# Dividing exponentials in plain column order, with a planner that knows the GpSimd port

## The chip, the cores and the metric

The kernel runs on one core of a Trainium2 chip. A core has five engines that take their instructions in order, each from its own queue: TensorE (PE in the profile, with its weight loads shown as PEld), VectorE (DVE), ScalarE (ACT), GpSimd (POOL), and SyncE (SP), which here only starts DMAs. The metric is the time of one execution on the device in microseconds; the time given for a kernel is the median of its runs.

## The reference

The input is a batch of 32 sequences of 256 tokens with 256 features, in fp32. Each sequence goes through a cross attention with 16 heads of 16 features between the sequence `x` and the side input, with a mask by length and one extra key per query (its own), then through a two-layer transformer, and the result is added to `x`. Cut to what matters here, a layer is:

```python
h = shift_token(x)                       # second half of the features from the token before
q, k, v = split(h @ wqkv)                # 8 heads of 64
q, k = rotary(l2norm(q) * qs, l2norm(k) * ks)
sim = q @ k.T                            # own window of 128 tokens and the one before, causal
attn = softmax(where(mask, -inf, sim))   # exponentials, divided by their sum
x = x + (attn @ v) @ wo
h = layernorm(shift_token(x)) * lg + lb
a, g = split(h @ w1 + b1)
x = x + (a * gelu(g)) @ w2 + b2
```

The change touches the division in `softmax`.

## The kernel before, in words

The 32 sequences are worked off in 16 groups of two. The kernel does not write its instructions out directly. It first records them in a `Plan`: a *unit* is a stretch of TensorE work (with a tiling of the array: `full`, or 2 or 4 tiles by `rows` or by `cols`), and each instruction on another engine is a *node* that hangs on a unit. `Plan.run` then plays the whole program through with prices per instruction (`price`), delays from engine to engine (`HOP`), buffers of each pool, the eight PSUM banks among them, and picks at each moment which unit TensorE takes next. What it picks decides the order in which `Plan.issue` emits all instructions, on all engines; that order is then kept. All instructions are emitted at one line, 567 of the kernel before, so the profile's groups differ by tile names, not by lines.

The choice among units that are ready is a score in `policy`: the unit's place in a nominal schedule (`u.stand`, from a `PERIOD` for each group, a stretch, and a number per unit from the tables `SHIFT`, `FIRST` for the first group and `FINAL` for the last two), a price for a change of tiling (`SWITCH`), a price for a backlog on the engines that it feeds, and a bonus for feeding them (`FEED`, capped by `MOST`), and a price on banks (`BANKS`). A unit that is marked soft (a full-size product) is emitted in column tiles when it follows a unit in column tiles, so the order also decides in how many pieces a product is issued. Copies recorded on `either` go to VectorE or ScalarE, whichever the plan finds free first. A table load is added on ScalarE whenever its functions need another table.

The names that matter below:
- In the cross attention: `cq`, `ck`, `cs`, `vals` are projections, `self` a small product (8 columns), `S` the scores (their row maxima `mx` are taken on VectorE), `nmT` their transposes, `ST` the scores again in the other orientation, `eT` their exponentials, `AV` the weighted sums, `ohT`, `turn` transposes, `co` the output projection.
- In a layer's attention: `q`, `k`, `v` projections; `sq`, `rot`, `raw`, `ss`, `rq` the norm and the rotation (the products `raw<-raw,rot` and `raw<-raw,ss` and the powers `rq`, `ss` run on GpSimd); `qkT` transposes; `sc` the scores; `ex` the exponentials; `exT` their transposes; `av` the weighted sums; `wout` the output projection.
- In the feed-forward part: `mean`, `var` (1 column), `rs`, and `w` for the products with `w1` and `w2`.

The function `weights` makes the exponentials of two heads: the masked maximum on VectorE out of PSUM (`ex<-sc,misc`), the product of maximum and scale (`nm<-nm,rq`), the exponential on ScalarE with its sum (`den`), the reciprocal, and the division by the sum, in place in SBUF, on VectorE. The division goes through the columns in strided order: of 256 columns, or of 128, it takes one from each half in turn.

```python
part = (
    es[:, i, 1:3, :].rearrange("p k q -> p q k")
    if w
    else es[:, i, 0, :].rearrange("p (k q) -> p q k", k=2)
)
vec.tensor_scalar(part, part, den[:, i, w : w + 1], None, ALU.mult)
```

Of the kernel before, what the change touches and what calls it, by code (L numbers as in the profile page):

```python
# [14 lines left out]
AF = mybir.ActivationFunctionType  # L15
ALU = mybir.AluOpType
# [6 lines left out]
G = 2  # L23
# [125 lines left out]
class Node:  # L149


    def __init__(self, engine, unit, number):
        self.engine, self.unit, self.number = engine, unit or self, number
        self.ops, self.cost, self.table, self.load = [], 0.0, None, 0.0
        self.after, self.then, self.ready, self.tiles = {}, [], 0.0, set()


class Plan:
# [15 lines left out]
    def __init__(self, tc, engines, pools, make):  # L174
        self.tc, self.engines, self.pools, self.make = tc, engines, pools, make
        self.nodes, self.units, self.unit_, self.group, self.place = [], [], None, 0, 0.0
        self.stage, self.stages, self.done = 0, {}, set()


    def tile(self, pool, name, shape):  # L180
# [52 lines left out]
    def record(self, engine, name, args, kw):  # L233
# [6 lines left out]
        if engine == "PE":  # L240
            node, wide = u, int(np.prod(out.shape[1:]))
            u.soft = u.soft and name == "matmul" and kw["lhsT"].shape[1] == 128
            cost = (2 if name == "transpose" else 4) * (wide + 2) / 2400 / u.streams
            if name == "transpose" and u.streams > 1:
                cost = max(cost, 0.062 / u.streams)
            cost = max(cost, 0.2) if wide < 64 else cost
            u.small += wide < 64
            turn = 0.65 if name == "transpose" else 1.0 if wide >= 64 else 0.0
            u.weight += cost * turn * self.WORK.get(u.kind, 1.0)
            u.place += cost  # L250
            self.place += cost
        else:
            node = self.node(engine, u)
            self.edge(u, node)
            if name == "dma_start":

                dst, src = kw["out"].shape, kw["in_"].shape
                run = min(dst[-1], src[-1])
                cost, node.load = 0.55, int(np.prod(dst)) / run * max(0.048, run * 4 / 24e3) / 16
            else:  # L260
                cost, node.table = self.price(engine, name, args, kw, size)
                if engine == "X":
                    node.either = {"V": cost, "S": 0.068 + size / 1267}
                u.feeds[engine] = u.feeds.get(engine, 0.0) + cost
# [10 lines left out]
    def price(self, engine, name, args, kw, size):  # L275

        if engine in "VX":
            extra = 0.02 if name == "reciprocal" else 0.0
            if name == "scalar_tensor_tensor":
                extra = 0.06  # L280
            return 0.065 + extra + size / 960, "any" if engine == "X" else None
        if engine == "S":
            func = args[2] if name == "activation" else None
            table = "exp" if func is AF.Exp else "gelu" if func is AF.Gelu else "any"
            extra = 0.315 if "accum_out" in kw else 0.11 if table == "gelu" else 0.0
            extra += 0.09 if func is AF.Identity else 0.0
            return 0.068 + size / 1267 + extra, table
        power = any(v is ALU.pow for v in args)
        return (0.35 + 0.158 * size if power else 0.1 + (0.00187 if size <= 256 else 0.00215) * size), None

# [3 lines left out]
    def run(self, policy):  # L294
# [4 lines left out]
        units, self.backlog = [], {e: 0.0 for e in "VSGDX"}  # L299
        left = {n: len(n.after) for n in self.nodes}  # L300
        self.kind, self.table, pe, blocked = ("full", 1), "any", 0.0, 0.0
        self.begin()
        self.tick, self.filled, self.warm = 0, 0.0, False
        for n in self.nodes:
# [3 lines left out]
        for u in self.units:  # L308
            for tiles in u.takes.values():
                for t in tiles:  # L310
                    t.lead = u.cost if t.lead is None else t.lead
                tiles.sort(key=lambda t: t.lead)
        self.idle = self.switches = self.cold = self.wire = 0.0

        def put(n):
            if n.engine == "PE":
# [40 lines left out]
        while todo:  # L357
# [12 lines left out]
            if e != "PE":  # L370
                ready = [n for n in waiting[e] if n.ready <= t]
                n = min(ready, key=lambda n: self.rank(n, e))
                waiting[e].remove(n)
                cost = n.cost
                if e == "S" and n.table not in ("any", None, self.table):
                    self.table, cost = n.table, cost + 1.3
                now[e] = t + cost
# [3 lines left out]
                todo -= 1  # L381
                end = t + cost
                if n.load:
                    self.wire = max(self.wire, end) + n.load
                    end = self.wire + self.LANDING
                ended(n, end)
                continue
            fit = {u: fits(u) for u in units if u.ready <= t}
# [148 lines left out]

    def rank(self, n, e):
        other = e == "S" and n.table not in ("any", None, self.table)
        return n.ready + 2.0 * other, n.number  # L540


    def parted(self, u):
# [8 lines left out]
    def issue(self, order):  # L552
# [7 lines left out]
        for n in order:  # L560
# [3 lines left out]
            for name, args, kw in ops:  # L564
                if n.engine in "VS" and name == "copy":
                    name = "tensor_copy" if n.engine == "V" else "copy"
                ins = getattr(self.engines[n.engine], name)(  # L567
                    *[real(v) for v in args], **{k: real(v) for k, v in kw.items()}
                )
# [3 lines left out]
class Engine:  # L573
# [12 lines left out]


SHIFT = [
    156, 528, 54, -76, 49, 292, -28, 245, 120, -102, -425, 52, -30, 35, 68, 22, 33, 22, -208,
    -4, 119, -41, 61, 69, 90, 152, 19, 32, -62, -238, 52, -2, 49, -168, 13, -85, -54, -65, 36,  # L590
    64, 112, -439, -349, -167, 223, -408, -5, 62, -46, -234, 56, -27, 119, -7, -45, 96, -17,
    -38, 61, -374, -335, -58, 1, -150, -372, -152, -51, -265, -409, 8, 67, -53, 114, -41, -17,
    -83, 34, 68, 48, 60, -261, -99, -7, -76, -335, -100, -105, -191, -306, -58, 15, -102, 32,
    -23, -66, 39, -309, -188, 106, -258, 33, -30, -139, 22, -141, 82, -290, -255, 32, 19, -99,
    134, 126, 14, -15, -222, -574, -156, 97, 93, -32, -241, 50, 152, -118, -41, -45, 21, -102,
    20, 47, 3, 15, 55, 169, -56, -24, 43, 199, -247, 143, -97, -15, -223, -41, -95, -88, -212,
    -127, -29, -32, -285, -545, -142, -265, -8, -118, -6, 152, 84, -122, 25, 14, 4, 18, 141, 60,
    166, -454, -139, 25, -127, -186, -20,
]
FIRST = [  # L600
    0, 0, 0, 0, 0, 0, 0, 0, 10, 35, -9, 213, 102, 95, 210, -345, -65, -122, -290, 49, -201, 6,
    -193, -61, -7, 106, 99, -6, -100, -16, 106, 13, 65, -266, -137, 7, -58, 247, 58, 69, 48, 1,
    -114, -155, -32, -173, -34, 65, 135, 130, -117, 69, 71, 117, 272, 156, 73, -3, -1, -31, -33,
    -133, 51, 151, 175, 239, 445, 215, 231, 120, 135, 97, -3, -90, -188, -357, -32, -64, -276,
    -297, -374, -330, -535, -346, -72, -135, -217, 156, 27, 182, 40, -174, -48, 77, -252, -118,
    -307, -246, 33, -96, -400, -238, -150, -69, -239, 6, 79, 152, 26, -38, -60, -358, -15, -155,
    89, -99, -69, -60, 87, -3, -114, -222, -118, 60, -143, -246, -29, -171, -319, -115, -49,
    -17, -96, -75, -88, 113, 144, -56, -6, 35, -9, -141, -41, -74, -183, -115, -131, -49, -79,
    109, -65, -145, 55, -88, -244, -157, -153, -264, -181, -118, -121, -82, -23, -37, -86, -83,
    -110, -213, -219, -209, -160, -63, 0, 0,  # L610
]
FINAL = [
    0, 0, 0, 0, 0, 0, 0, 0, 56, -34, 24, 16, 12, 140, -55, -63, -14, 1, -33, -84, -66, -53, -46,
    -145, -40, -121, 67, -19, -32, -29, 98, 97, 8, 45, -119, -130, -61, -106, 67, 94, -33, 8,
    54, 33, 8, -94, -222, -47, -210, -95, -90, -11, -121, 156, 49, 10, 43, 87, 7, 64, -144, -81,
    35, -80, 47, -31, -76, -182, 53, 86, 32, 67, 229, 49, 115, 31, 6, -10, -135, 40, 27, -79,
    -83, -8, 108, -110, 63, -40, -249, -98, -95, -18, -170, -139, -28, -12, -41, 76, 83, 116,
    59, -9, 65, -157, -74, -50, -119, -145, -16, -25, 13, 6, 73, -2, -181, -184, -151, -49, -97,
    116, -8, 56, 187, 15, 69, -31, -42, -59, 109, 161, 193, 112, 209, 211, 117, 80, 41, 59, 77,
    -84, 136, 47, 92, -54, 145, 66, 93, 1, -60, 152, -30, 108, 108, -119, 50, -9, -29, -39, 44,  # L620
    -113, -118, -128, -103, 66, 10, -89, -27, -49, -2, -10, 53, 34, -67, -8,
]


# [1 line left out]
def tile_kernel(ctx: ExitStack, tc: tile.TileContext, a: dict, out: bass.AP):  # L626
# [415 lines left out]
    def attention(l, b, res):  # L1042
# [80 lines left out]
        def weights(c, sc):  # L1123
# [29 lines left out]
                        accum_out=den[:, i, w : w + 1],  # L1153
                    )
            vec.reciprocal(den, den)

            for i in range(2):
                for w in range(2):
                    part = (
                        es[:, i, 1:3, :].rearrange("p k q -> p q k")  # L1160
                        if w
                        else es[:, i, 0, :].rearrange("p (k q) -> p q k", k=2)
                    )
                    vec.tensor_scalar(part, part, den[:, i, w : w + 1], None, ALU.mult)
            return es

        def turned(ess):
# [209 lines left out]
    STRETCH, AHEAD, LAST = 2.75, 3, 14  # L1377
    AGE, SWITCH, OVER, STAY, ENTER = 0.02, 1.5, 1.0, 6.0, 4.0
    HURRY = 0.0
    FEED, MOST, BANKS = 1.0, 3.0, 0.0  # L1380


    numbers = {}
# [68 lines left out]
```

## Time and profile before

| what | value |
|---|---|
| median of three runs | 3427.64 us (3423.55 to 3428.22) |
| the profiled execution's own time | 3422.27 us |
| its span, first to last instruction | 3420.5 us |
| mean granted TensorE clock | 0.990 |
| TensorE busy | 3348.6 us (98%) |
| VectorE busy | 2161.9 us (63%) |
| ScalarE busy | 1780.5 us (52%) |
| GpSimd busy | 1163.4 us (34%) |
| ScalarE table loads | 96, 1283 ns each |

A group of the profile is one kind of instruction with its tiles: busy time, mean duration, and the engine's idle time before them. A busy TensorE is not one at its peak, since the ends of matmuls are modelled; the distance from the start of one matmul to the start of the next says more. An fp32 product appears as two records in the profile, a transpose as one.

### The profile page before, as it was taken

What the parts mean: (1) busy time and instruction counts of PE and PEld (TensorE: products, weight loads), DVE (VectorE), ACT (ScalarE), POOL (GpSimd) and SP (SyncE); (2) the same over time, 40 slices, a digit from 0 to 9 for tenths busy, and PEclk for the clock granted to TensorE, in tenths of its full rate; (3) what the DMA queues carried; (4) which work ended last, traced back from release to release, by engine and by line L of the source; (5) the groups of instructions that cost most, each with busy time, mean ns of one, the idle gap of its engine ahead of it and who ended that gap; (6) DMA issues with size and microseconds to landing.
All of it is one profiled execution on the core that took longest, in us unless ns stands there. A gap on an engine that the chain in (4) does not pass through costs nothing.

```text
span 3420.5 us, 69279 instructions
## 1 busy us (share of the span) xinstructions
PE 3348.6 (98%) x25984; PEld 1908.7 (56%) x25984; DVE 2161.9 (63%) x6673; ACT 1780.5 (52%) x4537; POOL 1163.4 (34%) x1195
## 2 busy tenths in 40 slices
PE   6999999999999999999999999999999999999998
PEld 5665556465564655656455564655646556465554
DVE  3558567485675747657485674847657486574763
ACT  0556456473554726456373563735547364554653
POOL 0325052250613407043160522507134070432541
PEclk7999999999999999999999999999999999999999
DMA  5100010010101001010010100101010010100001
GB/s 147 20 15 11 12 27 9 16 26 9 26 15 21 17 13 20 16 20 17 13 21 14 27 13 15 24 7 26 16 20 17 13 20 15 27 15 12 4 2 27
DMA packets 310926, 69.00 MB, mean 20 GB/s; under 512 B 286776, under 2 KB 308096, under 8 KB 310592
## 3 DMA queue, kind: packets, MB, share of 16 engines
q1 hardware_dynamic: 298848, 54.24, 9.3%
q10 hardware_dynamic: 11744, 10.34, 1.1%
q8 instruction: 207, 3.39, 0.4%
q14 instruction: 127, 1.04, 0.1%
HBM read 35.53 MB, written 8.39 MB: 13 GB/s over the span
## 4 chain that ended last, share of the span: by engine, by line
PE 77%; DVE 12%; POOL 3%; ACT 1%; issue 1%; POOLq 0%; SPq 0%; DMA 0%; DVEq 0%; ACTq 0%
PE w L567 27%; DVE ex L567 6%; PE wout L567 6%; PE q L567 5%; PE av L567 4%; PE k L567 4%; PE sc L567 4%; PE S L567 4%; PE v L567 3%; PE ST L567 3%; PE vals L567 3%; PE AV L567 3%; PE exT L567 2%; PE qkT L567 2%; DVE rot L567 2%; PE cs L567 2%
## 5 line engine op out<-in xcount | busy, mean ns | idle before, releaser
L567 ACT ACTIVATE ex<-ex,nm,rq 128x128 f32<-128x128 f32 (+1 forms) x1024 | 546.2, 537 | 107.3 <-DVE nm L567 106.1
L567 PE MATMUL w<-cen,w 128*128 128x512 f32 (+2 forms) x1480 | 589.2, 598 | 0.8 <-DVE cen L567 0.3
L567 POOL TENSOR_TENSOR raw<-raw,rot 128x512 f32<-128x512 f32 x256 | 327.6, 1281 | 749.2 <-DVE rot L567 660.3
L567 PEld LDWEIGHTS w<-cen,w 128*128 128x128 f32 (+2 forms) x1480 | 224.9, 175 | 270.7 <-issue 231.4
L567 DVE TENSOR_SCALAR ex<-ex,den 128x128 f32<-128x128 f32 (+1 forms) x1024 | 351.4, 457 | 5.2
L567 DVE TENSOR_REDUCE mx<-S 128x2 f32<-128x512 f32 x512 | 314.3, 686 | 49.4 <-PE S L567 49.3
L567 PE MATMUL w<-act,w 128*128 128x512 f32 (+3 forms) x880 | 324.6, 602 | 2.9 <-DVE act L567 2.8
L567 ACT ACTIVATE eT<-ST 128x512 f32<-128x512 f32 x512 | 263.8, 605 | 115.0 <-PE ST L567 109.8
L567 DVE CUSTOM_DVE_ANT_0 ex<-sc,misc 128x128 f32<-128x128 f32 (+1 forms) x1024 | 299.2, 353 | 31.3 <-PE sc L567 30.8
L567 DVE SCALAR_TENSOR_TENSOR act<-w,b,act 128x512 f32<-128x512 f32 (+1 forms) x192 | 143.4, 748 | 262.0 <-PE w L567 195.5
L567 ACT ACTIVATE act<-w,b 128x512 f32<-128x512 f32 (+1 forms) x192 | 128.9, 686 | 280.1 <-PE w L567 276.8
L567 POOL TENSOR_TENSOR xs<-stream 128x512 f32<-128x512 f32 x32 | 35.0, 1094 | 641.5 <-PE cs L567 318.1
L567 PE MATMUL wout<-qT,wout 128*64 128x256 f32 (+2 forms) x1728 | 242.8, 381 | 0.5 <-DVE nm L567 0.3
L567 PE MATMUL v<-wqkv,stream 128*128 128x512 f32 (+1 forms) x608 | 242.5, 599 | 0.0
L567 PE MATMUL k<-wqkv,stream 128*32 128x512 f32 (+2 forms) x1104 | 239.9, 593 | 0.0
L567 PE MATMUL q<-wqkv,stream 128*32 128x512 f32 (+2 forms) x960 | 237.7, 594 | 0.2 <-ACT stream L567 0.2
L567 ACT COPY exT<-exT 128x384 f32<-128x384 f32 x512 | 207.3, 498 | 54.5 <-PE exT L567 53.8
L567 PEld LDWEIGHTS w<-act,w 128*128 128x128 f32 (+3 forms) x880 | 124.8, 176 | 167.1 <-issue 151.5
L567 POOL TENSOR_TENSOR rq<-ss,minus_half 128x8 f32<-128x8 f32 x128 | 215.1, 1684 | 4.9
L567 POOL TENSOR_TENSOR ss<-ss,minus_half 128x8 f32<-128x8 f32 x128 | 213.3, 1666 | 5.7
L567 PE MATMUL sc<-kT,qT 64*128 64x128 f32 (+1 forms) x2048 | 205.7, 337 | 0.4
L567 PEld LDWEIGHTS wout<-qT,wout 128*64 128x64 f32 (+2 forms) x1728 | 161.6, 147 | 73.0 <-issue 17.6
(127 smaller groups left out, 5520.2 us busy)
## 6 DMA issues: line engine op xcount, KB each, us to landing
ft<-in_fside_BxSxS_dram SPq DMA_DIRECT2D x128, 64.0 KB
xt<-in_x_dram SPq DMA_DIRECT2D x128, 64.0 KB
qh<-qc SPq DMA_DIRECT2D x256, 32.0 KB
kh<-kc SPq DMA_DIRECT2D x256, 32.0 KB
ot<-in_x_dram SPq DMA_DIRECT2D x128, 64.0 KB
out_dram<-ot SPq DMA_DIRECT2D x128, 64.0 KB
wqkv<-in_L_ffn_wqkv_dram ACTq DMA_DIRECT2D x2, 1536.0 KB
w<-in_L_ffn_w_dram ACTq DMA_DIRECT2D x2, 1364.0 KB
```

Source lines behind the costliest of these rows:

```text
L567: ins = getattr(self.engines[n.engine], name)(*[real(v) for v in args], **{k: real(v) for k, v in kw.items()})
```

## The change

Three things change.

- The division runs over the columns in plain order, on the same data.
- The planner learns about a port. A VectorE `tensor_scalar` or `scalar_tensor_tensor` with no operand in PSUM (`node.port`) waits in the plan for a GpSimd instruction of 64 columns or more (`node.holds`) to end. It also prices the division at half as much per column as before, GpSimd's `tensor_scalar` at 0.205, and lets at most eight DMAs be under way at once. An operation `scaled` is understood and not used, and a term `hurry` is added to the rank with the factor 0.
- The order of units is found anew: other numbers in `SHIFT`, `FIRST` and `FINAL`, and other values of `FEED`, `MOST` and `BANKS`. With it the order of nearly all instructions changes on all engines.

```diff
@@ class Plan, record
                 cost, node.table = self.price(engine, name, args, kw, size)
+                inside = [v for v in views if not v.tile.pool == "bank"]
+                two = name in ("scaled", "scalar_tensor_tensor", "tensor_scalar") and size >= 4
+                node.port = engine in "VX" and two and len(inside) == len(views)
+                node.holds = engine == "G" and size >= 64
@@ class Plan, price
+            if name in ("tensor_scalar", "scaled") and args[0].tile.pool != "bank" and size >= 64:
+                return 0.128 + size / 1920, None
             return 0.065 + extra + size / 960, "any" if engine == "X" else None
...
+        if name == "tensor_scalar":
+            return 0.205, None
@@ class Plan, run
                 cost = n.cost
+                if n.port and e == "V":
+                    t = max(t, held)
+                elif n.holds:
+                    held = t + cost - 0.12
...
                 if n.load:
-                    self.wire = max(self.wire, end) + n.load
+                    at = max(t, self.landed[-8]) + cost
+                    now[e] = at
+                    self.wire = max(self.wire, at) + n.load
                     end = self.wire + self.LANDING
+                    self.landed.append(end)
@@ class Plan, rank
-        return n.ready + 2.0 * other, n.number
+        return n.ready + 2.0 * other + self.hurry * n.unit.stand, n.number
@@ SHIFT, FIRST, FINAL: all numbers (the first of each shown)
-    156, 528, 54, -76, 49, 292, -28, 245, 120, -102, -425, 52, -30, 35, 68, 22, 33, 22, -208,
+    284, 905, -274, -314, -462, 111, -423, -52, 159, 0, -640, 27, 4, 52, 147, -5, 19, -365,
...
@@ weights
             for i in range(2):
                 for w in range(2):
-                    part = (
-                        es[:, i, 1:3, :].rearrange("p k q -> p q k")
-                        if w
-                        else es[:, i, 0, :].rearrange("p (k q) -> p q k", k=2)
+                    vec.tensor_scalar(
+                        flat[i][w], flat[i][w], den[:, i, w : w + 1], None, ALU.mult
                     )
-                    vec.tensor_scalar(part, part, den[:, i, w : w + 1], None, ALU.mult)
@@ policy's constants
-    FEED, MOST, BANKS = 1.0, 3.0, 0.0
+    FEED, MOST, BANKS = 1.5, 5.0, 1.0
```

## The prediction

> **What bounds the kernel now.** I read the page's busy shares first, then the longest pieces of the chain of waits, then the waits of TensorE, the groups by form, and last the timeline at single places. The busy shares and the slices:
>
> ```profile
> span 3420.5 us, 69279 instructions
> PE 3348.6 (98%) x25984; PEld 1908.7 (56%) x25984; DVE 2161.9 (63%) x6673; ACT 1780.5 (52%) x4537; POOL 1163.4 (34%) x1195
> PE   6999999999999999999999999999999999999998
> PEclk7999999999999999999999999999999999999999
> ```
>
> TensorE (PE) is busy all the time outside the first and the last slice, at the full granted clock. VectorE (DVE), which the edit relieves, has a third of its time free. So a faster DVE is worth only what PE waits for it, and the order of PE's own instructions is worth whatever it costs directly. The chain shows how regular the middle is: the same 16-record piece returns every 207.2 us.
>
> ```profile
> 977.80 7.13 PE w L567 x16
> 1184.96 7.13 PE w L567 x16
> 1392.20 7.13 PE w L567 x16
> ```
>
> What PE waits for (the view names the last releaser; the list is long, these are the entries of the repeating part that matter):
>
> ```profile
> PE exT L567 <- ACT sq L567: 5.5, 11, 0.5
> PE turn L567 <- POOL at L567: 4.5, 13, 1.5
> PE ck L567 <- DVE nm L567: 3.4, 11, 1.0
> PE qkT L567 <- DVE rot L567: 2.7, 11, 0.3
> ```
>
> Columns: us in total, times, longest. They are about one stall per group each, all in the attention part. Two places of the timeline show what the edit speaks of: four divisions of a 128x128 block, once beside a wide GpSimd (POOL) instruction and once without one.
>
> ```profile
> 1115.30 2.18 DVE L567 TENSOR_SCALAR ex<-ex,den 128x128 f32<-128x128 f32 x4
> 1115.26 1.27 POOL L567 TENSOR_TENSOR raw<-raw,rot 128x512 f32<-128x512 f32 x1 [1.73 <-DVE den L567]
> 1143.57 1.17 DVE L567 TENSOR_SCALAR ex<-ex,den 128x128 f32<-128x128 f32 x4
> ```
>
> The first four start 0.04 us after the POOL instruction and take 1.01 us more than the other four: they stand until it is done. So the strided order of columns does not keep the kernel of before out of this contention.
>
> **The division in plain order.** 512 divisions of 128x128 at 396 ns and 512 of 128x256 at 518 ns:
>
> ```profile
> L567 DVE TENSOR_SCALAR ex<-ex,den 128x256 f32<-128x256 f32 x512 | 263.8, 518 | 0.0
> L567 DVE TENSOR_SCALAR ex<-ex,den 128x128 f32<-128x128 f32 x512 | 203.0, 396 | 5.2
> L567 POOL TENSOR_TENSOR raw<-raw,rot 128x512 f32<-128x512 f32 x256 | 327.6, 1281 | 749.2 <-DVE rot L567 660.3 <-DVE den L567 76.3 <-DVE nm L567 12.6
> ```
>
> In the trace's single records an undisturbed strided one starts its successor after 183 ns (128 columns) and 293 ns (256): about 1 ns a column. The nearest row in plain order is the copy of qh from misc at the start, 2048 columns in 1.21 us, 0.59 ns a column; by it a column gets cheaper by about half, 0.066 and 0.133 us. At most 512 x 0.199 = 102 us of DVE time, 6.4 a group; at least nothing. I take 90. None of it is on the path: PE covers it, and if that cover were gone it would be worth 6.4 us a group.
>
> On the mode itself: the Trainium skill, "VectorE: DVE Perf Modes", section "Mode 2×_2P", has single-source fp32 work between SBUF tensors run two results a cycle whenever the outermost dimension is even; by it the strided form had that rate already and the edit would give nothing. The 293 ns for 256 columns disagree, and the sum goes by the rows.
>
> **The port.** Of the 128x128 divisions, 353 had no POOL work beside them (mean 328 ns), 97 lay beside a wide POOL instruction for over 0.3 of their time (mean 687); of the 128x256, 46 lay so (961 against 475); of the 128x4 products nm<-nm,rq, 39 (454 against 157). The excess is 97 x 0.36 + 46 x 0.49 + 39 x 0.30 = 69 us of DVE, 4.3 a group. DVE instructions that read PSUM show no excess (the masked maximum of 256 columns: 421 beside POOL, 420 alone), nor do those beside the powers of 128x8. This is what the new `port` and `holds` say, so the planner now sees delays that it didn't: it can save between none and all of the 69 us of DVE; I take half. POOL's own 1163 us stay: same instructions.
>
> The Trainium skill, "SBUF — State Buffer", section "Who interferes with whom", speaks against the edit: `tensor_scalar` in its two-port mode and GpSimd exclude each other for a whole instruction, so plain order would bring contention, of either side; the pair of timelines above shows it there already.
>
> **The new order, the part that costs.** The built programs can be counted, and the counts priced by the spacing of PE's records in the trace: each run of like matmuls is its number times a spacing, plus a seam to the next run that depends on the two tilings; medians over the whole trace leave stalls out.
> - The same work in another tiling is nearly free: a 512-column product takes 0.865 us at full tiles, 2 x 0.429 in two column tiles, 4 x 0.214 in four; 256 columns 0.436 against 2 x 0.216. More of them at full tiles: +2.
> - The little products (self, 8 columns; var, 1 column) aren't: 0.75 us a unit at full tiles, 0.43 in two column tiles.
>
> ```profile
> 1009.52 0.59 PE L567 MATMUL self<-misc,prod 128*64 128x8 f32 x16
> 1009.95 1.92 PE L567 MATMUL w<-cen,w1t 128*64 128x512 f32 x8
> 2907.68 0.95 PE L567 MATMUL self<-misc,prod 128*128 128x8 f32 x8
> 2908.57 1.15 PE L567 MATMUL ST<-qh,kh 18*128 18x256 f32 x16
> ```
>
> Full-tile units go from 14 to 48, two-tile ones from 46 to 14: 34 x 0.75 - 32 x 0.43 = +12.
> - Changes of tile shape go from 1064 to 1147, each 0.09 to 0.2 us, and seams between full-tile runs of different width from 259 to 340 at 0.075: together +16.
> So PE back to back takes 3262 us before and 3291 after, +30. In the part that repeats, the same sum gives 202.8 us a group before and 205.5 after. This term is the surest of the forecast.
>
> **The new order, the part that pays.** Before, a group takes 207.2, so 4.4 us beyond back to back; about 3.5 of it are stalls at qkT, sc, exT, turn and at the unit after them, in the attention part where DVE and POOL are behind. Over the whole run it is 139 us: some 51 up to 107 us (loads, and half clock: the granted clock is 0.61 from 30 to 60 us and 0.70 from 60 to 100), 17 more up to 430, 40 in the nine equal groups, the rest beside them and at the end. The new order leaves more PE work between a unit and the one that needs its result. In one repeating group, by the same spacings, smallest and median in us: ST to AV 2.1 and 5.0 before, 3.9 and 7.7 after; sc to exT 9.2 and 12.4, then 8.5 and 15.5; AV to ohT 1.8 and 2.1, then 2.5 and 2.8; wout to mean 2.6 and 3.6, then 5.0 and 8.3. With DVE relieved by up to 6.4 + 4.3 a group as well, I take the 4.4 down to 1.4 (bounds 0.5 and 4.4): 206.9 a group, -0.3, or -3 over nine groups (bounds -11 and +24).
>
> Outside them back to back grows by 30 - 9 x 2.7 = +5, against some 99 us lost there. At the start the new order does all projections of the second sequence before the first S, where PE waited 4.5 and 2.9 us; but then eight S units follow each other, each with four maxima of DVE (2.49 us the four) against about 1 us of PE. The first ST, at 85.9 us before, comes at about the same time. Then there is more slack up to 430 and at the end. I take -17 for the waits outside (bounds -35 and +8), so -12 there.
>
> **Smaller things.** ACT loads its tables 140 times, not 96: 44 x 1.28 = +56 us, 3.5 a group, covered by ACT's idle 48%; without that cover up to 3.5 a group. 21 copies of aT go from DVE (0.69) to ACT (0.58); 18 of kT follow and 22 of qT<-av go the other way: a wash. DMAs are the same 1316 on SP, some in another order; `landed`, the price of the POOL tensor_scalar and `hurry` (0.0) only shape the plan. Below nothing the table loads can't go, since they only occupy ACT; the copies can, by as much as they cost.
>
> **Sum.** -3 - 12 = -15 on the profiled execution's 3422.3, which stands 5.4 below the median of the runs, 3427.6: I give the change on the median, 3413.
>
> **Rivals.**
> - The stalls stay (slower). The 4.4 us are banks and GpSimd results that the division has no part in (exT waits for ACT, turn for POOL), and the 3.5 us of table loads fall among the exponentials. Then PE's +2.7 a group comes through whole: 9 x 2.7 + 5 = +30, 3458; half of it, 3442. It decides once less than 2.7 of the 4.4 goes. For it: sc to exT got tighter at its smallest. Against: the measured excess of 69 us at the port, and the wider medians.
> - The trade cancels: stalls fall by just what the tilings cost, and the start gives nothing: 3421 to 3434.
> - More than I take: waits down to 0.5 a group (-11) and -35 + 5 outside: -41, 3387.
> - The division isn't faster in plain order (the rule above): the plan, which prices it at half a column, is late by 6.4 us of DVE a group; worth some +0.5 a group in waits, so it lies inside the first two.
>
> **How the numbers follow.** The forecast's case (3395 to 3420) has 0.45, the deeper gain 0.07, the cancelled trade 0.2, the stalls that stay 0.28. About 0.2% (6.9 us) is what a measurement of this kernel can tell from no change: faster 0.51, same 0.21, slower 0.28. The range cuts the deepest gains and the top of the slower case: 3388 to 3447.
>
> **What would show it.** Right: the repeating piece returns every 206.5 to 207; division rows near 300 and 360 ns; 140 table loads; PE's waits in the attention part down by more than half. Wrong: a period of 208.5 or more; division rows as before; new PE waits on ACT exT or eT behind table loads; a first ST later than 95 us.

## The result and the profile after

The changed kernel takes 3431.01 us (median of 16 runs, 3427.39 to 3438.47); the kernel before took 3423.66 beside it (16 runs, 3418.93 to 3429.11). The ratio is 1.0022, with a 95% interval of 1.0015 to 1.003: 7.4 us slower, where 15 us faster was forecast. The profiled execution took 3429.14 us.

The page of the kernel after, the same lines as were shown of before:

```profile
span 3427.4 us, 66848 instructions
PE 3372.4 (98%) x24870; PEld 1952.6 (57%) x24870; DVE 2131.9 (62%) x6658; ACT 1839.8 (54%) x4596; POOL 1163.7 (34%) x1195
PE   8999999999999999999999999999999999999998
PEclk7999999999999999999999999999999999999999
```

PE is busy 23.8 us longer, DVE 30 us shorter. The clock is as before, so the loss is in what PE does. The chain of waits of the kernel after (start, length, piece) shows the length of a repeating group:

```profile
1023.77 11.36 PE w L591 x26
1233.40 11.36 PE w L591 x26
1443.03 11.36 PE w L591 x26
1652.66 11.36 PE w L591 x26
```

The piece returns every 209.6 us, against 207.2 before: 2.4 us more in each of nine groups, some 21 in all. The rest of the run therefore gained: 7.4 - 21 = -14. The period of before is itself not quite fixed: one of its nine groups took 207.9 us, and in another execution of the same program (`b_bare` below) five of nine took 207.9 to 208.0, a mean of 207.6. By that run the nine groups lose 18 us and the rest gains 11. What PE waits for, in the kernel after (us in total, times, longest):

```profile
PE v L591 <- ACT sq L591: 12.2, 11, 1.1
PE cq L591 <- DVE fT L591: 11.8, 3, 8.6
PE bias L591 <- DMA bq<-in_L_cond_bq_dram: 7.5, 1, 7.5
PE w L591 <- DVE cen L591: 1.1, 2, 0.6
```

The four stalls that stood in every group before (exT 0.5, turn 0.25, ck 0.2, qkT 0.25 us in a usual group, 1.2 together) are gone as entries of every group, and one of 1.1 us stands in their place. Outside the nine groups the list adds up to 47 us before and to 28 after: that is where the rest of the run gained. The history of the new stall in the timeline of one group, after:

```profile
1515.11 1.21 POOL L591 TENSOR_TENSOR tv<-vs,es 128x256 f32<-128x256 f32 x2
1515.72 1.62 DVE L591 SCALAR_TENSOR_TENSOR nm<-nm,rq 128x4 f32<-128x4 f32 x1
1516.26 1.05 POOL L591 TENSOR_TENSOR raw<-raw,ss 128x512 f32<-128x512 f32 x1
1517.37 0.49 ACT L591 ACTIVATE ex<-ex,nm,rq 128x128 f32<-128x128 f32 x1 [1.06 <-DVE nm L591]
1523.76 0.58 ACT L591 ACTIVATE sq<-q 128x512 f32<-128x512 f32 x1
1524.39 1.98 PE L591 MATMUL v<-wqkv,stream 128*128 128x512 f32 x4 [1.12 <-ACT sq L591]
```

A product of four columns takes 1.62 us on DVE (the next ones: 0.15 and 0.13), and it ends just after two POOL instructions that follow each other have ended: it stands behind both. The exponentials that need it start late and run on ACT back to back until 1523.76. The copy `sq` behind them empties a PSUM bank too late, and PE stands 1.12 us. Two experiments below (`a_pool`, `a_nm`) break this chain at two places, and the stall goes in both.

The groups by form of the kernel after show that the division did get faster:

```profile
L591 DVE TENSOR_SCALAR ex<-ex,den 128x256 f32<-128x256 f32 x512 | 193.2, 377 | 0.0
L591 DVE TENSOR_SCALAR ex<-ex,den 128x128 f32<-128x128 f32 x512 | 165.9, 324 | 4.3
L591 DVE SCALAR_TENSOR_TENSOR nm<-nm,rq 128x4 f32<-128x4 f32 x256 | 61.6, 247 | 0.7
```

### The profile page after: what moved, and what is told of

The parts are those of the page before. It is cut to its first block, busy times and chain, and to the rows that moved or that the text cites. A ratio compares the mean times of both kernels' runs of the same rounds, so it can differ in the third digit from the quotient of the medians.

```text
span 3427.4 us, 66848 instructions
## 1 busy us (share of the span) xinstructions
PE 3372.4 (98%) x24870; PEld 1952.6 (57%) x24870; DVE 2131.9 (62%) x6658; ACT 1839.8 (54%) x4596; POOL 1163.7 (34%) x1195
## 4 chain that ended last, share of the span: by engine, by line
PE 88%; DVE 4%; ACT 3%; POOL 1%; issue 1%; DVEq 0%; POOLq 0%; ACTq 0%
PE w L591 27%; PE wout L591 6%; PE v L591 6%; PE q L591 6%; PE k L591 5%; PE av L591 5%; PE sc L591 5%; PE ST L591 4%; PE S L591 4%; PE AV L591 3%; PE vals L591 3%; PE exT L591 3%; ACT ex L591 2%; PE qkT L591 2%; DVE ex L591 2%; PE cq L591 2%
## 5 line engine op out<-in xcount | busy, mean ns | idle before, releaser
L591 PE MATMUL w<-cen,w 128*128 128x512 f32 (+2 forms) x2032 | 580.9, 595 | 1.1 <-DVE cen L591 1.1
L591 PE MATMUL w<-act,w 128*128 128x512 f32 (+3 forms) x804 | 331.6, 608 | 0.0
L591 DVE TENSOR_SCALAR ex<-ex,den 128x128 f32<-128x128 f32 (+1 forms) x1024 | 295.6, 351 | 4.3
L591 PE MATMUL v<-wqkv,stream 128*128 128x512 f32 (+2 forms) x604 | 247.6, 605 | 12.2 <-ACT sq L591 12.2
L591 PE MATMUL k<-wqkv,stream 128*128 128x512 f32 (+2 forms) x752 | 241.9, 594 | 0.0
L591 PE MATMUL wout<-qT,wout 128*128 128x256 f32 (+2 forms) x1424 | 241.2, 382 | 0.2 <-PE S L591 0.2
L591 PE MATMUL q<-wqkv,stream 128*128 128x512 f32 (+2 forms) x624 | 239.0, 597 | 0.4 <-ACT stream L591 0.4
L591 POOL TENSOR_TENSOR ot<-ot,yt 128x512 f32<-128x512 f32 x32 | 40.4, 1267 | 525.5 <-DVE yt L591 448.1
```

The lines of the kernel that those rows point to most:

```text
L591: ins = getattr(self.engines[n.engine], name)(*[real(v) for v in args], **{k: real(v) for k, v in kw.items()})
```

## The experiments

Two theories stood after the result. Theory 1: the new order costs PE what the spacings said (+2.7 us a group), and next to nothing was saved in waits, because most of the 4.4 us that I had called waits were never waits. Theory 2: the waits were there and were saved, and something else came instead (table loads, the faster division meeting the port, new stalls). Periods below are the distance between the same pieces in the nine repeating groups, and "the spacings" are the sum of the prediction (number of matmuls by spacing, plus seams) for the order in question. The intervals leave 3 to 6 us either way in a time (13 in `b_free` and `a_cols2_free`, of two executions each), so a difference of two times is good to 4 us at best; the periods of the groups are much steadier.

### The division, alone and taken back

In the order after, the strided form is put back; in the order before, the plain form is put in:

```diff
# a_strided: the changed kernel's division as it was before; b_plain: the reverse in the kernel before
-                    vec.tensor_scalar(
-                        flat[i][w], flat[i][w], den[:, i, w : w + 1], None, ALU.mult
-                    )
+                    part = (es[:, i, 1:3, :].rearrange("p k q -> p q k") if w
+                            else es[:, i, 0, :].rearrange("p (k q) -> p q k", k=2))
+                    vec.tensor_scalar(part, part, den[:, i, w : w + 1], None, ALU.mult)
```

> The changed kernel with the division alone put back into strided order; the order of all instructions stays that of the changed kernel (the plan goes on pricing it as plain). Theory 1, TensorE's own order sets the time and the division is covered: VectorE gets some 75 us busier, the repeating group stays near 209.6 us (up to 210.1), the time within +0.25% of the changed kernel's 3431, so 3431 to 3440. Theory 2, the division in plain order pays for much of the order's cost: 211 us a group or more, over 3445.

Measured: 3428.95 us (ratio to before 1.0017, 1.0008 to 1.0025), 209.65 a group. The division's rows are 506 and 369 ns, from 377 and 324, and the time does not get longer: in the order after the faster division is worth nothing.

> The kernel before with the division alone in plain order, all instructions in the order of before. Theory 1: the four stalls of a group (1.3 us of idle TensorE) shrink at most a little; 206.7 to 207.2 us a group, 3416 to 3424. Theory 2, VectorE's lateness is what TensorE waits for: 206 us a group or less, 3410 or less. The port can also turn it round (the faster form meets GpSimd at other moments): up to 3428.

Measured: 3418.99 us (0.9988, 0.9979 to 0.9997), 206.9 a group. In the order before, the division is worth some 4 us (1 to 7): the stall of ck behind the product nm goes from 3.4 to 2.1 us, 0.2 in each group. That stall comes and goes: in the kernel before, run again as `b_bare`, it is 6.5 us, and the groups in which it lasts 0.9 to 1.0 us are those of 207.9 to 208.0. In the profile with the plain division no group has it. So this part of the change was a small gain, and the order is what lost.

Three further runs were meant to cut the other engines' work in the attention part to eight columns, in the orders of before, of after, and of `a_cols2` (below). The cut reached only operands with two axes: the division in plain order, and in the kernel before no instruction at all. They say nothing of the waits they were made for.

```diff
# b_bare, a_bare, a_cols2_bare, shortened to what the cut came to (in b_bare: nothing)
+                if n.engine != "PE" and args[0].tile.name in (..., "ex", ...) and name == "tensor_scalar":
+                    args = tuple(v[:, 0:8] if v.shape == wide else v for v in args)
```

> The order before, with TensorE's instructions unchanged and the other engines' work cut: the copies into eT, exT, kT, qT and aT, the division, the rotation's two inputs rot and GpSimd's raw write 8 columns only (everything behind them computes on what lay there). TensorE is left nearly without waits, so the group shows its own time. The forecast's reading (the 4.4 us a group beyond back to back are waits): 202.8 to 204.0 a group. Rival (some 1.3 of it are waits, the rest is TensorE's own, in seams that the sum of spacings misses): 205.6 to 206.0.

> The same cuts in the order after. The forecast's reading: 205.5 to 206.7 a group. Rival: 208.2 to 208.6. The difference of the two kernels' groups is then what the new order costs TensorE by itself: 2.7 by the forecast, 2.4 if it equals the whole measured difference of 209.6 and 207.2 , which would mean that the new order took no waits away in the group.

> The same cuts in the order after with every soft product in two column tiles, whose group was forecast at 206.5 to 207.5 from spacings of 202.6 and took 208.0. If TensorE's own time is what missed (seams inside the cut products): 206.6 to 207.0, some 1.0 to 1.4 below 208.0 as in the other two. If the products did arrive and new waits ate them: 203 to 205.

Measured: 3423.61 us (0.9997, 0.9987 to 1.0006: the kernel before once more), 3432.68 (1.0024, 1.0014 to 1.0033; 209.5 a group) and 3405.94 (0.9943, 0.9928 to 0.9958; 207.9 a group, where `a_cols2` has 208.0). In the group by form of a_bare the division is down by 163 us, from 193.2 + 165.9:

```profile
L595 DVE TENSOR_SCALAR ex<-ex,den 128x8 f32<-128x8 f32 x1024 | 196.2, 259 | 4.3
```

DVE as a whole was busy 94 us less, and the time stayed within 2 us of the changed kernel's: even a division of eight columns does not shorten it. Only under the two-column tiles did the cut give something, some 6 us, of which the nine groups have about 1.

### The tilings: is the cost of back to back real?

The order after with nothing changed but the tiling of products. `a_small`: self and var in two column tiles (48 units). `a_cols2`: every soft product so. `a_full`: every soft product at full tiles.

```diff
             if n.engine == "PE" and n.soft and n.tiling[0] == "cols":
                 ops = self.parted(n)
+            elif n.engine == "PE" and n.soft and n.ops and n.stage[0] >= 0:   # a_small: and n.small == len(n.ops)
+                n.tiling = ("cols", 2)
+                ops = self.parted(n)
# a_full, instead: n.tiling = ("full", 1) for the soft units, ahead of the first test
```

> The changed kernel with all small products (self, 8 columns; var, 1 column) issued in two column tiles as most of them were before; 48 units change, nothing else moves. Priced 0.75 us a unit at full tiles and 0.43 in two column tiles, less the seams of a change of tiling (0.1 to 0.2 us where the neighbours are full): theory 1 says -4 to -15 us, 3416 to 3427, and 0.3 to 1 us less a group (three such units in it). If TensorE waits anyway (theory 2), nothing: 3431.

Measured: 3418.83 us (0.9986, 0.9978 to 0.9995), 209.0 a group: 12.2 less than the changed kernel, give or take 4, where 4 to 15 were expected. That PE waits anyway (nothing, 3431) is excluded.

> The opposite: every soft unit of the changed kernel at full tiles. By the spacings TensorE back to back rises from 3291 to 3317, a group from 205.5 to 206.7. Theory 1: 210.5 to 211 us a group, 3446 to 3460 in all. Theory 2, slack takes it: within 5 us of 3431.

Measured: 3449.14 us (1.0084, 1.0069 to 1.0099), 210.6 a group: 1.0 more a group (spacings 1.2) and 18 in all (spacings 26).

> The changed kernel with every soft unit (projections, feed-forward, small products) issued in two column tiles, whatever it follows; units and all other instructions stay in their order. By the spacings of the trace of before TensorE back to back falls from 3291 to 3251 us, a repeating group from 205.5 to 202.6. Theory 1, TensorE's own order sets the time: 206.5 to 207.5 us a group and 3385 to 3400 in all. Theory 2, what TensorE saves comes back as waits for the other engines: 209 us a group and over 3420.

Measured: 3411.60 us (0.9963, 0.9952 to 0.9975), 208.0 a group. That is 19.4 less than the changed kernel, half of the 40 that the spacings say, and 12 less than the kernel before: the fastest of the kernels here that still do all the work. It lies between the two expectations, so it decides for neither alone. Four kernels with one order of units stand in the order that the spacings give them: the tiling is a direct cost. The sum is right within the noise for small products, and overrates what the large ones in pieces give back.

The same tiling in the order before, with the plain division (`b_cols2p`, both edits as above):

> The order before, the plain division, and every soft product in two column tiles. By the spacings of TensorE's matmuls back to back falls from 3261.7 to 3247.8 us (group 202.8 to 202.4), -14; the plain division gave -5 in this order alone. Theory 1 (sizes as measured so far: about half of what the spacings say arrives): 3408 to 3414 against about 3423, a group of 206.3 to 206.8. Rival (seams between tilings are real and arrive in full, and stalls get no cover): 3400 to 3408 . Rival (nothing arrives, since two tiles only help the order after): 3417 to 3421.

Measured: 3414.49 us (0.9976, 0.9966 to 0.9985), 207.2 a group. The gain is 4.5 us beyond the plain division's, a third of the spacings' 14, and none of it in the repeating group (206.9 with the plain division alone, where 206.3 to 206.8 were expected here).

### GpSimd, the port and the tables

GpSimd's sums and products of the rotation cut to one head of eight (the other heads stay unrotated and unscaled), in both orders:

```diff
# a_pool, b_pool
+                if n.engine == "G" and name == "tensor_tensor" and args[0].tile.name == "raw":
+                    args = (*[v[:, 0:1] for v in args[:3]], *args[3:])
```

> The changed kernel with GpSimd's sums and products on raw cut to one head of eight (the other heads are left unrotated or unscaled): 384 of its wide instructions shrink from 1.0 to 1.3 us to about 0.25. That takes most of the port's hold and of GpSimd's lateness away. Theory 1: only the stall before v can go, 208.4 us a group and 3413 to 3425. Theory 2, the port and GpSimd set the time in many small waits: 206 us a group or less, under 3400.

Measured: 3418.72 us (0.9985, 0.9973 to 0.9996), 208.6 a group; the stall of v behind sq falls from 12.2 to 1.7 us in all, as in the expectation of Theory 1:

```profile
PE v L593 <- ACT sq L593: 1.7, 11, 0.2
```

The product of four columns now takes 0.77 us at most, where 12 of its 256 took over 1 us. So the group gets back 1.0 us, about the 0.95 by which its one listed stall shrank.

> The order before, with GpSimd's products and sums of the rotation cut to one head of eight (the other heads stay unrotated and unscaled). Theory 1 (of the 4.4 us a group beyond back to back, only the stalls that are seen as waits can go, about 1.3 us, the rest is seams that the spacings miss): group 205.7 to 206.5, 3405 to 3415 against about 3423. Rival (the port and GpSimd cause most of the 4.4, as the forecast took it): group 203.3 to 205, 3385 to 3403.

Measured: 3389.22 us (0.9907, 0.9891 to 0.9922), 206.0 a group. In the group the two orders give up nearly the same, 1.2 us before and 1.0 after: Theory 1 there. In the whole run they don't: 34 us before, which is the rival's range, and 12 after. So the new order is less exposed to GpSimd, but the difference lies outside the repeating part. Near the end, for instance, the cut shortens the order before by 9.2 us (from its 32-record piece of w to its last one, 244.9 to 235.7) and the order after by 3.4 (from its 16-record piece at 3072.4 to its last one, 304.9 to 301.5).

The product behind the port in the changed kernel, made as four products of one column:

```diff
# a_nm
+                if name == "scalar_tensor_tensor" and args[0].tile.name == "nm" and ...:
+                    for w in range(2):
+                        for i in range(2):
+                            col, by = (real(v[:, w, i : i + 1]) for v in (args[0], args[3]))
+                            self.engines["V"].tensor_scalar(col, col, by, -1.0, ALU.mult, ALU.mult)
+                    continue
```

> The changed kernel with the product nm<-nm,rq of 128x4 issued as four products of one column with a scalar each, which read one SBUF tensor and are too small for the faster mode; all else in order. In the changed kernel's trace this product stands 1.6 us beside two GpSimd instructions, the exponentials start late, ScalarE runs 6.4 us of them in a row, and the v unit behind them waits 1.1 us for a bank: the one stall of its repeating group. If that chain is right, the stall goes, 208.5 us a group and 3416 to 3422 in all; if the four products wait for the port too, or ScalarE is late for another reason, 209.6 and 3429 to 3433.

Measured: 3439.46 us (1.0047, 1.0034 to 1.006), 209.5 a group. The stall of v is gone, so the chain was read rightly. But in the waits of this run another of the same size has its place, and the whole takes 8 us more:

```profile
PE wout L598 <- DVE qT L598: 11.0, 11, 1.0
```

This does not show that the removal is worth nothing. The four products cost DVE more than the one (1024 of 202 ns, 142 us busy, in place of 61.6), 5 us more a group, and the new stall is one behind DVE; `a_pool` takes the same stall away without that cost and gains 1.0 us a group. No run takes the stall away and leaves the load of both DVE and GpSimd as it was.

The table loads, with Gelu replaced by Square, which needs hardly any (the gates' values are then not the reference's):

```diff
# a_tables
+                if name == "activation" and args[2] is AF.Gelu:
+                    args = (*args[:2], AF.Square)
```

> The order after, with the gates' Gelu replaced by Square, which leaves ScalarE without most of its table loads (the gates' values differ from the reference's). Theory 1 (the 140 table loads lie in ScalarE's idle time, as the forecast had it): same as the changed kernel within 4 us, 3427 to 3433, group 209.3 to 209.7. Rival (they sit among the exponentials and hold TensorE's units back, up to 3.5 us a group): 3390 to 3415, group 206.5 to 208.8.

Measured: 3435.02 us (1.0036, 1.0022 to 1.005), 209.6 a group. The group is the changed kernel's to a tenth, so the table loads (1 in this run, 140 in the changed kernel) cost it nothing. The 4 us more in all lie outside the repeating part; in the profile they stand in the start, with the first ST 74.2 us after the first matmul in place of 70.2.

### Parts of the order

`h_mix` takes the changed kernel's numbers and prices for the first group and the last two, and those of before between them, with the plain division:

```diff
# h_mix
+            u.mid = 1 <= s[0] < 14
+            shift, first_, final = (SHIFT_B, FIRST_B, FINAL_B) if u.mid else (SHIFT, FIRST, FINAL)
...
-                    s -= FEED * min(k / u.cost, MOST)
+                    s -= (1.0 if u.mid else FEED) * min(k / u.cost, 3.0 if u.mid else MOST)
```

> One plan with the changed kernel's tables, constants and prices for the first group and the last two, and those of before for the groups between (division plain throughout). Its repeating groups have the back-to-back time of before, 202.8 us by the spacings. Theory 1: 207.2 us a group in the middle, and the ends as in the changed kernel, which is some 8 us ahead of before when the repeating part begins and gains some 9 behind it: 3424 - 17 = 3407 (3400 to 3415). Rival: the ends gain only in that order as a whole, or the seams between the two orders cost it: 3420 to 3430.

Measured: 3439.5 us (1.005, 1.0038 to 1.0063). The middle is at 206.9 to 207.0 a group, but the joints cost more than the ends gain: the first of the equal groups begins 17 us later than in before (cq at 966.7 us, from 949.4), and the two steps from group to group behind the last one take 220.1 and 193.9 us, from 204.5 and 182.6. The gain at the ends was not taken out of the order this way; whether joints found for it would keep it is open.

`a_oldtab` is the other half: the changed planner with `SHIFT`, `FIRST`, `FINAL` and the policy's constants of before.

> The change without its new numbers: plain division and the planner's new prices and port, with the tables and policy constants of before; the plan then gives a third order. By the spacings back to back is 3287.9 us, 205.4 a repeating group (before 202.8, changed 205.5). Theory 1 (the cost of back to back arrives and the stalls stay): group 209 to 210, in all 3440 to 3460, as the ends were not found anew for it. Rival (the planner that knows the port takes the stalls out by itself, and the new numbers are what costs): group 206 to 207, 3405 to 3425.

Measured: 3505.49 us (1.0242, 1.0225 to 1.026), 209.5 a group. The group is as Theory 1 has it; the whole is far beyond both expectations, with some 78 us more beyond its spacings (3505 - 3288) than the changed kernel has beyond its own (3431 - 3291), most of it at the end: in the profiles it is 14 us behind the changed kernel at the last product cq and 80 behind at the end. Old numbers under new prices don't tell what the planner's model of the port is worth by itself, and that stays open.

### TensorE without results to wait for

What decides between the theories is how long PE takes when it waits for no result. PE's instructions keep their order and shape, but each operand that another engine makes in the course of the work is replaced by a part of a weight that lies in SBUF from the start. Only qh, kh and vh of the cross attention, which DMAs and DVE fill, were left as they are, so the expectations' "every operand" says a little too much. Nothing that is computed reaches the next product, and in the groups PE waits for PSUM banks and little else. The products keep their pace: the piece of 24 records of w takes 10.30 us in before too, the one of 26 records 11.36 in the kernel after.

```diff
# b_free, a_free, a_cols2_free
+                if n.engine == "PE":
+                    args = (*args[:1], *[self.steady(v) for v in args[1:]])
+                    kw = {k: self.steady(v) if k in ("lhsT", "rhs", "in_") else v for k, v in kw.items()}
```

> The order before, with TensorE's instructions in the same order and of the same shapes, but every operand that another engine makes in the course of the work is replaced by a part of a weight that lies in SBUF from the start. TensorE then waits for no result, only for a PSUM bank to be emptied (the output is not the reference's: nothing that is computed reaches the next product). The forecast's reading (the 4.4 us a group beyond back to back are waits for results): 202.8 to 203.8 a group. Rival (some 1.3 of it are waits, the rest is TensorE's own time, in seams that the sum of spacings misses): 205.6 to 206.0.

> The same for the order after. The forecast's reading: 205.5 to 206.5 a group. Rival: 208.2 to 208.6. The difference between the two kernels' groups is what the new order costs TensorE by itself: the forecast said 2.7; the whole measured difference is 2.4 (209.6 and 207.2).

> The same for the order after with every soft product in two column tiles, whose group was forecast at 206.5 to 207.5 from spacings of 202.6 and took 208.0. If the missing part is TensorE's own (seams inside the cut products): 206.6 to 207.0, some 1.0 to 1.4 below 208.0. If the gain did arrive and new waits ate it: 203 to 205.

Measured: 3391.14 us (0.9899, 0.9861 to 0.9937), 3415.47 (0.9967, 0.9952 to 0.9982) and 3395.22 (0.9911, 0.9876 to 0.9946). The chain of waits of b_free gives 205.7 us a group:

```profile
1023.01 10.30 PE w L585 x24
1228.63 10.30 PE w L585 x24
1434.27 10.30 PE w L585 x24
```

That of a_free gives 209.2:

```profile
1021.46 11.36 PE w L609 x26
1230.66 11.36 PE w L609 x26
1439.87 11.36 PE w L609 x26
```

The waits of TensorE in b_free name what is left in each group, late banks:

```profile
PE exT L585 <- ACT sq L585: 5.5, 11, 0.5
PE qkT L585 <- DVE rot L585: 2.5, 11, 0.3
PE sc L585 <- DVE nm L585: 1.7, 10, 0.2
```

In a_free the list has one such entry:

```profile
PE v L609 <- ACT sq L609: 18.6, 11, 1.7
```

These are 0.5 + 0.23 + 0.17 = 0.9 us a group before and 1.7 after (each total divided by its times). Taken off, PE's own time is 205.7 - 0.9 = 204.8 before and 209.2 - 1.7 = 207.5 after; for the two-column tiles it is 207.2 - 1.3 = 205.9. These are upper bounds, since waits of under 0.15 us are in no list.

| us a group | before | after | difference |
|---|---|---|---|
| sum of spacings | 202.8 | 205.5 | +2.7 |
| PE's own time (free runs less bank stalls) | 204.8 | 207.5 | +2.7 |
| waits of all kinds (period less own time) | 2.4 | 2.1 | -0.3 |
| period | 207.2 | 209.6 | +2.4 |

Theory 1 holds in what it says of the cost: the +2.7 is PE's own, and next to nothing was saved in waits. Its reason holds only in part. Of before's 4.4 us beyond the spacings, 2.0 are PE's own, the same in both orders, so the spacings give the difference of two orders well and their level badly; what those 2.0 us are made of no run shows. The other 2.4, more than half, were waits, and in the new order there are 2.1 again: they fell by 0.3, not by 3 (by 0.7 if the mean of 207.6 in `b_bare` is taken for before). The list of waits shows only 1.2 of the 2.4 and 1.1 of the 2.1. The rest are short ones at many places. The kernel after and a_free have the same PE records in the same order, and set against each other the step from q to co takes 0.59 us in the first and 0.43 in the second, the one from exT to cq 0.36 and 0.15. Of the rivals' numbers on record, b_free's came in; a_free's 209.2 lies above the 208.2 to 208.6 expected and a_cols2_free's 207.2 above 206.6 to 207.0, as the late bank now holds PE up for 1.7 and 1.3 us (1.1 in the kernel after; presumably since PE comes to it earlier). In the two-column tiles PE's own time fell by 1.6 of the 2.9 that the spacings say, and the period by the same 1.6: what was missing there was PE's own as well, not new waits.

## Why the prediction was wrong, point by point

- **The step that failed is "I take the 4.4 down to 1.4".** It rested on the larger intervals between a unit and the one that needs its result and on the relieved DVE. Beyond the spacings 4.1 us are left after the change. There were two errors in it. The 4.4 was the difference between a period and a sum of medians, and I read all of it as waits, 3.5 of it as stalls at named places; 2.0 of it was PE's own time, and the new order has the same 2.0. The waits view was a warning: its entries for the repeating part came to 1.2 us in a usual group. And of the 2.4 us that were waits, the new order took one set away and made another of 2.1, with the stall of v (1.1) as its largest. So wider intervals and a lighter DVE moved the waits and hardly shortened them.
- **The +2.7 us a group, the surest term, came as forecast**, in the sum, in the free runs and in the tiling runs. The +12 of the small products measured 12.2, give or take 4.
- **The period** was to be 206.9, and 208.5 or more was to mean wrong; it is 209.6.
- **The ends** were to give -12 (17 us of waits less, 5 more of back to back) and gave -11 to -14, by the run that the period of before is taken from. The lists have 19 us of waits less there, 12 of them in the first 430 us. The first ST, which was to come at about the same time, stood at 70.2 us after the first matmul in the profiled run, from 78.1 before; this start differs by several microseconds from run to run of one order (69 to 74 in the runs of the order after, 75 to 85 in those of before), so the split of the 19 us is rough.
- **The division**: rows of 377 and 324 ns, where near 360 and 300 were to show it right; 108 us of DVE less in those two groups, where 90 were taken, at most 102. With the order held, against `a_strided`, it is 512 x (129 + 45) ns = 89 us, so the term was sized rightly, and the other 19 came with the order. That PE covers it held.
- **The port**: half of the 69 us of excess was to go. By the same count the excess after is some 63: 61 of the 128x128 divisions beside a wide POOL instruction at 0.38 us too much, 22 of the 128x256 at 0.73, 46 products nm at 0.52. Fewer divisions are caught, each for longer, and more of the products on which exponentials wait. The excess hardly fell. What the plan's model of the port is worth by itself no run shows.
- **The table loads** were 140, and free, as taken.
- **The rival "the stalls stay"** had the outcome in the groups: back to back comes through nearly whole, and the waits stay about as large, at other places. It too took all of the 4.4 for stalls, and it counted the table loads among them, which cost nothing. Its price of +30 had +5 at the ends, where the change gained 11 to 14. The figure itself fell into the range of the cancelled trade (3421 to 3434), but that is luck: in the groups the waits did not fall by what the tilings cost, and at the ends, where that rival expected nothing from the start, the gain paid for most of it.

On the rule of the Trainium skill weighed in the prediction ("VectorE: DVE Perf Modes", section "Mode 2×_2P": two results a cycle for one fp32 source in SBUF, with an even outermost dimension): putting the strided form back raised the rows by 129 and 45 ns with the same order, so these runs disagree with it for the strided form. The strided form also waits for GpSimd like the plain one: its 128 columns took 707 ns beside wide POOL instructions and 323 without in `a_strided`, the plain ones 661 and 278 in the kernel after. On the other page weighed there ("SBUF — State Buffer", section "Who interferes with whom": a VectorE instruction with two inputs in SBUF contends with a GpSimd instruction that reads SBUF), the 1.62 us of the four-column product beside POOL instructions agree; here it stood until they had ended, however little it moves.

## What to carry to other kernels

Before counting on stalls to go, separate them from the busy engine's own time: give that engine operands that need no wait and time it so. A sum of spacings told these two orders apart to a few tenths of a microsecond a group, but its distance to the measured time is not an account of waits: 2.0 of 4.4 us were none. The list of waits is a lower bound, here about half of them. And a new order that takes the listed stalls away can bring others of the same size, so count what it brings as well: here it was 2.4 us a group before and 2.1 after.

## What the runs showed of the hardware

- A division of eight columns still takes 259 ns on average in the order after (324 for 128 columns, 377 for 256); with no POOL work beside it it takes 222 (277 and 346), so the columns are the smaller part of it at this size.
- The one-column form of the product nm by `tensor_scalar` does not stand behind GpSimd: 202 ns beside wide POOL instructions and 202 without, where the four-column `scalar_tensor_tensor` of the kernel after takes 679 beside them and some 150 alone.
- Products of 8 columns at full tiles cost more than in two column tiles: the eight self products at full tiles took 0.95 us in the kernel after, and the sixteen half ones 0.64 in `a_small`, in the same place of the order.
